# Context projection drawn into a state-space layer, state sums put ahead of a convolution, and a small copy put first in a chunk

## The chip, the cores and the metric

The kernel runs on one core of a Trainium2 chip. The metric is device time in microseconds (us), the median of several executions. A core has five engines with one instruction queue each: TensorE (PE, matrix products, results in PSUM), VectorE (DVE), ScalarE (ACT), GpSimd (POOL) and SyncE (SP, which here only issues DMA transfers). Engines run side by side and wait for each other by semaphores; within one queue the order is fixed.

## The reference, cut to what matters

All arrays are float32. The image x has 2 batches of 128 channels of 64x64 positions. Four layers follow each other:

- Layer 0: a layer norm over channels, then four Mamba passes over the 4096 tokens of each batch (row order forward and backward, column order forward and backward), each with a projection to 256 channels, a causal convolution of four taps, a scan over 16 states, a gate and an output projection; the four outputs are fused and added to x.
- Layer 1: attention of each position over a context picture, and a 3x3 convolution of the result, added to x.
- Layer 2: attention of x over itself, added to x.
- Layer 3: a small Mamba over groups of 16 channels, a group norm, and an addition.

The context has 4 pictures of 256 channels of 32x32. It is resized bilinearly to 2 pictures of 64x64 and then multiplied by Wk and Wv:

```python
ctx = jax.image.resize(context_feat, (B, Cc, H, W), method='bilinear')
q = conv2d(sr_feat, Wq, bq, 0).reshape(B, C, H * W)
k = conv2d(ctx, Wk, bk, 0).reshape(B, C, H * W)
v = conv2d(ctx, Wv, bv, 0).reshape(B, C, H * W)
```

Resizing and projecting are both linear. The kernel therefore first mixes the 4 pictures to 2 (weights 3/7, 3/7, 1/7 and 1/7, 3/7, 3/7), projects at 32x32, and resizes the 128 projected channels in height and width last. The context does not depend on x.

## The kernel before, in words

**Layer 0.** The work is cut into 64 chunks of 512 tokens: batch, then order (row or column), then direction, then 8 pieces. Chunk k has 16 steps; step u treats one group of 4 states (u%8//2) and one quarter of the 256 channels. The channels of a quarter and its states fill 128 partitions, so a step works on 128x1024. In each step POOL forms dbu (L330), ACT the decay da (two halves, L343), a correction of the first token (s_fix, L358) and the carried state (s_hst, L379); DVE scans (s_scan, L374); the product with C is on DVE (s_hc, L386), in five of the sixteen steps on POOL (L384); PE sums over states (s_y, L397) and spreads C over partitions (s_pc, L363).

Around the steps lies what prepares other chunks. For the chunk after next: px, the projection with the convolution folded in, as four shifted products (L228), in two halves px(0) and px(1), each copied out by ACT (x_, L237), and then pd (L267), which makes the 73 rows of the inputs of dt, B and C. For the next chunk: xd_ (L272), which copies these 73 rows out of PSUM and stores B and C to DRAM, pt (L287), dt and its product (L306, L314), and the gate's projection pz (L241). For the chunk before: the gate product yg(0) and yg(1) (L404) and the output projection po (L415, L419). For later chunks, in 11 chunks, a layer norm: center, sub, square, var, rows, scale, mul, affine. In 16 chunks ACT transposes a strip of the normed tokens (turn, L201) from xn to xnt, which the column-order chunks read.

The order is written out by hand. For each chunk the dictionaries A (ACT), V (DVE), M (PE) and G (POOL) say what is issued in which step besides the fixed work, and the loop over s issues it. A norm goes on in a chunk where ln is not None (it begins) or lp is not None (it ends). The results of px, pz, pd, pt, center, var, scale and po share one PSUM bank (misc), so each must be copied out before the next may start. y has one bank as well; y0 starts it at steps 3 and 11.

**The crossing to layer 1.** Behind the last chunk, weights m1 and m2 are loaded on SP (L682, L683), the product of two weight matrices wvo and a bias bo are formed (L705 to L710), the four context pictures are loaded (L726), mixed on DVE (L731 to L733), projected in 32 PE records (L740), copied out by ACT (L742), and stored with doubled edge rows to DRAM (L746).

**Layers 1 and 2.** Four jobs (layer, batch) of 16 groups of 256 queries are run through 16 slots each, as a pipeline: scores of one group (L847), probabilities and values (L902) of the one before, sums of the one before that. A key piece or a value piece of 1024 positions is made from the low picture by a load (L799), a wide part on ACT and POOL (L804 to L813) and a high part on ACT and POOL (L818 to L824); value pieces are also transposed on PE (L785). The first two key pieces come before the first slot, the others at slots given to piece.

Of the kernel before, what the change touches and what calls it, by code (L numbers as in the profile page):

```python
# [13 lines left out]
P = 128  # L14
B, C, H, W = 2, 128, 64, 64
L = H * W
T = 512
# [39 lines left out]
def conv_seq_kernel(ctx: ExitStack, tc: tile.TileContext, a: dict, out: bass.AP):  # L57
# [13 lines left out]
    for b in range(B):  # L71
        for lo, hi in ((0, 1), (1, 2), (2, 4), (4, 8)):
            sl = slice(lo * T, hi * T)
            nc.sync.dma_start(x[:, b, sl], xin[:, b, sl])
# [14 lines left out]
    nc.vector.tensor_scalar(aneg, aneg, -1.0, None, ALU.mult)  # L89

# [3 lines left out]
    with ExitStack() as c0:  # L94
# [22 lines left out]
        nc.scalar.dma_start(w_dt[64:ND, :], a["wdt"])  # L117
        w_xT, w_out, w_fT = mt[:, 0:256], mt[:, 256:512], mt[:, 512:1024]
# [21 lines left out]
        for t in (xn, xnt):  # L140
            nc.vector.memset(t[:, 0:3], 0.0)
            nc.vector.memset(t[:, L + 3 : L + 6], 0.0)

# [292 lines left out]
        turns = {k: k % 8 for k in (*range(6, 14), *range(32, 40))}  # L436
# [6 lines left out]
        with tc.manual_schedule():  # L443
# [64 lines left out]
            for i in range(2):  # L508
                nc.vector.tensor_scalar(diag_d[:, i, :], ident, v(f"dp{i}"), None, ALU.mult)
            for j in (2, 3):  # L510
                act(sqs[j], xcs[j], AF.Square)
# [20 lines left out]
            nc.vector.reciprocal(r[:, 8:16], r[:, 8:16])  # L532
            for i in range(2):
                c1.px(i, ba[i])
# [21 lines left out]
            for k, c in enumerate(chunks):  # L556
# [15 lines left out]
                if new is not None:  # L572
                    A[0] = (new.xd_,)
# [9 lines left out]
                if nxt is not None:  # L583
                    M[8], A[9] = lambda: nxt.px(0), (lambda: nxt.x_(0),)
                    M[10], A[12] = lambda: nxt.px(1), (lambda: nxt.x_(1),)
                    A[13] = (nxt.xsilu,)
                    M[15] = nxt.pd
                if lp is not None:
# [3 lines left out]
                    A[10] = (lp.affine,)  # L592
                if ln is not None:
                    M[12], V[13] = ln.center, ln.sub
                    A[14] = (*A.get(14, ()), ln.square)
                    M[14], A[15] = ln.var, (ln.keep,)
                if k in turns:
                    A[11] = (lambda: turn(turns[k]),)

                for s in range(16):  # L600
# [11 lines left out]

                    if c1 is not None:
# [7 lines left out]
                    if s in (3, 11):  # L621
                        c.y0(s // 11)
                    for cy, e in ((c, s), (old, s + 16)):
                        for u in pairs.get(e, ()) if cy is not None else ():
                            cy.s_y(u)
                            cy.s_y(u + 1)
# [35 lines left out]
    nc.sync.dma_start(m3, a["m3"])  # L662
    nc.sync.dma_start(cw3, a["cw3"].partition_broadcast(P))
    nc.sync.dma_start(dtw3, a["dtw3"].partition_broadcast(P))
# [4 lines left out]
    with ExitStack() as c1:  # L669
# [8 lines left out]
        dr = c1.enter_context(tc.tile_pool(name="dr1", bufs=1, space=bass.MemoryType.DRAM))  # L678

        m1 = gt([P, 1792], "m1", wp)  # L680
        m2 = gt([P, 512], "m2", wp)
        nc.sync.dma_start(m1, a["m1"])  # L682
        nc.sync.dma_start(m2, a["m2"])  # L683
        w1qT = m1[:, 0:128]
        w1kT = m1[:, 128:384].rearrange("p (k c) -> p k c", k=2)
        w1vT = m1[:, 384:640].rearrange("p (k c) -> p k c", k=2)
# [12 lines left out]
        def small(tag, shape, bufs=None):  # L699
# [4 lines left out]
        pw = misc()  # L704
        mm(pw[:, :P], lhsT=w2v, rhs=w2oT, start=True, stop=True)  # L705
        nc.vector.tensor_copy(wvo, pw[:, :P])
        bo = gt([P, 1], "bo", wp)
        pw = misc()
        mm(pw[:, :1], lhsT=w2oT, rhs=v("bv2"), start=True, stop=True)
        nc.vector.tensor_add(bo, v("bo2"), pw[:, :1])  # L710
# [6 lines left out]


        low = [[dr.tile([P, 34, 32], F32, tag=f"low{b}{w}", name=f"low{b}{w}") for w in range(2)]
               for b in range(B)]  # L720
        cfeat = a["ctx"].rearrange("b (k p) h w -> p b k (h w)", p=P)
        with ExitStack() as cc:
            cx = cc.enter_context(tc.tile_pool(name="ctx", bufs=1))
# [3 lines left out]
            for b in range(B):  # L727

                wts = (3 / 7, 3 / 7, 1 / 7) if b == 0 else (1 / 7, 3 / 7, 3 / 7)
                mix = cx.tile([P, 2, 1024], F32, tag="mix", name="mix", bufs=2)  # L730
                nc.vector.tensor_scalar(mix, feat[b], wts[0], None, ALU.mult)  # L731
                nc.vector.scalar_tensor_tensor(mix, feat[b + 1], wts[1], mix, ALU.mult, ALU.add)
                nc.vector.scalar_tensor_tensor(mix, feat[b + 2], wts[2], mix, ALU.mult, ALU.add)  # L733

                for w, (wT, bias) in enumerate(((w1kT, v("bk1")), (w1vT, v("bv1")))):
                    t = cx.tile([P, 34, 32], F32, tag="lo", name="lo", bufs=2)
                    for hf in range(2):
                        pl = bank("s", bufs=4)
                        for k in range(2):
                            mm(pl, lhsT=wT[:, k, :], rhs=mix[:, k, hf * T : (hf + 1) * T],  # L740
                               start=(k == 0), stop=(k == 1))
                        act(t[:, 1 + 16 * hf : 17 + 16 * hf, :], pl.rearrange("p (h w) -> p h w", w=32),  # L742
                            AF.Identity, bias=bias)
# [804 lines left out]
```

## Time and profile before

The median of 3 runs is 6803.33 us (6800.08 to 6806.97). The profiled execution took 6810.44 us.

| | us |
|---|---|
| span of the profiled execution | 6808.7 |
| busy PE, DVE, ACT, POOL | 6005.6, 5524.3, 4461.8, 5362.4 |
| first scan of layer 0 | 57.15 |
| last matmul of layer 0 ends | 3480.54 |
| first score of layer 1 | 3523.67 |

The busy time is a sum over stages that are limited by different engines, so it has to be read by stage. In a row of the clock-ordered view, the first number is the start in microseconds from the start of the span, the second the duration of what the row gathers, then come engine, line, operation, the tiles written and read, and in brackets how long the engine was idle before and what released it. In a row of the view of waits, the three numbers are the sum, how often, and the longest, in microseconds.

### The profile page before, as it was taken

The page shows a single profiled execution, that of the slowest core. Times are in us where ns is not written, and L with a number is a line of the kernel's source. Part 1 is how long each engine was busy: PE and PEld are TensorE (multiplying, and loading weights), DVE is VectorE, ACT ScalarE, POOL GpSimd, SP SyncE. Part 2 cuts the span into 40 slices and gives each one's busy share as a digit, 9 for nine tenths or more (in the row PEclk, how much of TensorE's full clock was granted, in tenths as well). Part 3 has the DMA queues.
Part 4 walks back from the last instruction along what each step waited for, and adds up shares of the span by engine and source line. Part 5 has one row for each costly group of instructions (what it writes and reads, how often), then busy time and mean ns, then how long its engine had stood idle before and what let it go on. Part 6 is the DMA issues. An engine that isn't in the chain of part 4 may idle for free. (4 is left out here: it accounts for less than half of the span.)

```text
span 6808.7 us, 67303 instructions
## 1 busy us (share of the span) xinstructions
PE 6005.6 (88%) x20652; PEld 2821.7 (41%) x20652; DVE 5524.3 (81%) x4499; ACT 4461.8 (66%) x7666; POOL 5362.4 (79%) x2487
## 2 busy tenths in 40 slices
PE   8888888888888888888879999999999997888888
PEld 2222222222222222222238887787788884222222
DVE  7999999999999999999966665565566675787777
ACT  7887778877788777887745664555456564434342
POOL 6899998899999999999956664555566666777776
PEclk7777777777778777777779999999999998988888
DMA  6565655566566656665630000000000001222221
GB/s 170 138 149 145 157 145 140 137 154 150 141 159 152 157 143 154 150 154 146 148 93 2 4 4 1 1 1 1 1 1 13 1 1 61 75 71 72 90 75 67
DMA packets 352652, 616.51 MB, mean 91 GB/s; under 512 B 72473, under 2 KB 74786, under 8 KB 351650
## 3 DMA queue, kind: packets, MB, share of 16 engines
q1 hardware_dynamic: 351552, 610.44, 35.2%
q8 instruction: 162, 2.65, 0.2%
q14 instruction: 200, 1.64, 0.1%
q10 hardware_dynamic: 738, 1.78, 0.1%
HBM read 496.45 MB, written 115.47 MB: 90 GB/s over the span
## 5 line engine op out<-in xcount | busy, mean ns | idle before, releaser
L330 POOL TENSOR_TENSOR dbu<-dus,bs 128x1024 f32<-128x1024 f32 x1024 | 2404.0, 2374 | 157.0 <-DVE h L374 141.1
L374 DVE TENSOR_TENSOR_SCAN h<-da,hst,dbu 128x1024 f32<-128x1024 f32 x896 | 2094.3, 2345 | 77.8 <-ACT dbu L358 75.0
L343 ACT ACTIVATE da<-dts,aneg 128x512 f32<-128x512 f32 (+1 forms) x2048 | 1412.6, 690 | 443.7 <-DVE h L374 404.1
L890 POOL TENSOR_TENSOR sum<-sum,sc 128x1024 f32<-128x1024 f32 x384 | 906.8, 2362 | 496.7 <-ACT sc L885 493.1
L852 ACT COPY sc<-s 128x512 f32<-128x512 f32 x1024 | 598.1, 585 | 867.7 <-PE s L847 753.5
L859 DVE TENSOR_TENSOR mx<-mx,s 128x512 f32<-128x512 f32 x896 | 610.1, 681 | 569.5 <-ACT sc L852 568.5
L847 PE MATMUL s<-q,k 128*128 128x256 f32 x4096 | 1058.0, 382 | 11.7 <-ACT q L833 8.4
L902 PE MATMUL av<-sc,v 128*128 128x256 f32 x4096 | 1049.6, 379 | 2.3 <-ACT sc L885 2.3
L397 PE MATMUL y<-hc,cst 128*32 128x512 f32 x4096 | 811.3, 760 | 179.2 <-DVE hc L386 103.8
L386 DVE TENSOR_TENSOR hc<-h,pc 128x1024 f32<-128x1024 f32 x704 | 844.9, 1200 | 0.1
L847 PEld LDWEIGHTS s<-q,k 128*128 128x128 f32 x4096 | 781.2, 192 | 146.2 <-issue 36.6
L902 PEld LDWEIGHTS av<-sc,v 128*128 128x128 f32 x4096 | 769.1, 190 | 103.1 <-ACT sc L885 3.7
L384 POOL TENSOR_TENSOR hc<-h,cs 128x1024 f32<-128x1024 f32 x320 | 758.2, 2369 | 1.3 <-issue 1.3
L363 PE MATMUL pc<-xd,sel 16*128 16x512 f32 x1024 | 713.4, 788 | 4.8 <-DVE hc L386 4.1
L1217 POOL TENSOR_TENSOR A<-A,D 128x1024 f32<-128x1024 f32 x224 | 525.9, 2365 | 225.2 <-DVE D L1222 200.3
L882 DVE TENSOR_TENSOR sc<-sc,pm 128x1024 f32<-128x1024 f32 x512 | 620.9, 1214 | 0.9 <-PE pm L878 0.9
L885 ACT ACTIVATE sc<-sc 128x1024 f32<-128x1024 f32 x512 | 542.3, 1059 | 8.6 <-DVE sc L882 8.1
L287 PE MATMUL misc<-xd,w_dt 9*128 9x512 f32 x504 | 386.5, 855 | 155.1 <-ACT x L426 83.6
L1210 ACT ACTIVATE A<-dtr,aneg 128x1024 f32<-128x1024 f32 (+1 forms) x256 | 246.0, 1032 | 380.8 <-PE y L1242 363.0
L397 PEld LDWEIGHTS y<-hc,cst 128*32 128x32 f32 x4096 | 104.9, 117 | 745.6 <-issue 337.4
L1228 DVE TENSOR_TENSOR A<-A,q 128x1024 f32<-128x1024 f32 (+1 forms) x256 | 276.9, 1082 | 148.4 <-PE q L1194 148.2
L1194 PE MATMUL q<-xs,lb 32*128 32x512 f32 x896 | 331.5, 712 | 72.0 <-DVE D L1204 65.7
(263 smaller groups left out, 8078.4 us busy)
## 6 DMA issues: line engine op xcount, KB each, us to landing
dts<-ddt SPq DMA_DIRECT2D x512, 256.0 KB, 5.5
dus<-ddu SPq DMA_DIRECT2D x512, 256.0 KB, 5.1
bs<-rows SPq DMA_DIRECT2D x1024, 64.0 KB, 4.9
cs<-rows SPq DMA_DIRECT2D x1024, 64.0 KB, 3.3
ddt<-dt SPq DMA_DIRECT2D x128, 256.0 KB, 2.0
ddu<-dtu SPq DMA_DIRECT2D x128, 256.0 KB, 4.1
dtr<-ddt SPq DMA_DIRECT2D x448, 64.0 KB, 1.9
rx<-ddx SPq DMA_DIRECT2D x448, 64.0 KB, 1.9
```

The lines of the kernel that those rows point to most:

```text
L330: nc.gpsimd.tensor_mul(t, self.dus[q], _bc(self.bs[g], 1, [P, 2, T]))
L343: act(t[:, i, sl], self.dts[q][:, i, sl], AF.Exp, scale=an[:, g, 2 * q + i : 2 * q + i + 1])
L363: mm(t, lhsT=sel[32:48, 4 * g : 4 * g + 4, :].rearrange("p n d -> p (n d)"), rhs=self.xd[32:48, :], start=True, stop=True)
L374: nc.vector.tensor_tensor_scan(ho, ai, bi, init, ALU.mult, ALU.add)
L384: nc.gpsimd.tensor_mul(t, self.h[u], _bc(self.cs[gq(u)[0]], 1, [P, 2, T]))
L386: nc.vector.tensor_mul(t, self.h[u], _bc(self.pc[u // 2], 1, [P, 2, T]))
L397: mm(self.y[q // 2][r : r + 32, :], lhsT=sum4, rhs=self.hc[u][:, i, :], start=False, stop=(u % 8 >= 6), skip_group_check=True)
L847: mm(p[:, o, :], lhsT=j.k[m // 8][:, m % 8 * P : m % 8 * P + P], rhs=self.q, start=True, stop=True)
L859: nc.vector.tensor_max(self.mx, self.s[0][:, 0:2, :] if u == 1 else self.mx, self.p[u])
L882: nc.vector.tensor_sub(s, s, _bc(self.pm[:, :], 1, [P, 4, NQ]))
L890: nc.gpsimd.tensor_add(self.sum, self.s[0] if w == 1 else self.sum, self.s[w])
L902: mm(self.av, lhsT=self.job.v[m // 8][:, m % 8, :], rhs=self.s[u // 2][:, m % 4, :], start=(m == 0), stop=(m == 31))
```

## The change

1. The context is loaded in the opening of layer 0, into buffers not yet in use: the first and last picture into xnt, the two middle ones into buffers of h and dbu. DVE mixes them there in place (`mixed`). Four chunks, 7 to 10, each project one batch for keys or values in two halves on PE through the misc bank (`Low`), ACT copies each out, and SP stores it to DRAM. The weights and outputs of this stand in the space of x[:, 1], which is loaded at the tops of chunks 11 to 14 instead of in the opening. The turns of the first batch come two chunks later.
2. Of the crossing there remain the loads of m1 and m2, now behind or between the loads of the first two key pieces, and the making of key pieces. The other steps are removed or, for wvo, bo and layer 3's weights, moved to slots 50 to 52 of the attention. The resizes for the first batch's keys use DVE instead of POOL. Later key pieces begin one slot earlier; value pieces begin two slots earlier, with their transposes at the same slots as before.
3. In every chunk of layer 0, px(0) is issued in step 9 instead of 8, and x_(0) in step 10. The text of y0 and the sums stands ahead of ACT's work, which changes no order within a queue.
4. In step 0 of chunks in which no norm ends, xd_ is issued ahead of the decay, the fix and the carry.

```diff
-    for b in range(B):
-            nc.sync.dma_start(x[:, b, sl], xin[:, b, sl])
+        nc.sync.dma_start(x[:, 0, sl], xin[:, 0, sl])
...
+        w_kv = x[:, 1, 0:512].rearrange("p (w k c) -> p w k c", w=2, k=2)
+        nc.scalar.dma_start(x[:, 1, 0:512], a["m1"][:, 128:640])
...
+        cfeat = a["ctx"].rearrange("b (k p) h w -> p b k (h w)", p=P)
+        mix = [[xnt[:, 3 + 1024 * (2 * b + k) : 1027 + 1024 * (2 * b + k)] for k in range(2)]
+               for b in range(B)]
+        feat = {}
+        for k in range(2):
+            nc.sync.dma_start(mix[0][k], cfeat[:, 0, k])
+        for j in (1, 2):
+            for k in range(2):
+                feat[j, k] = wt("h" if j == 1 else "dbu", NH if j == 1 else NDBU, (P, 1024))
+                nc.sync.dma_start(feat[j, k], cfeat[:, j, k])
+        for k in range(2):
+            nc.sync.dma_start(mix[1][k], cfeat[:, 3, k])
+
+        def mixed(b):
+            w = (3 / 7, 3 / 7, 1 / 7) if b == 0 else (1 / 7, 3 / 7, 3 / 7)
+            for k in range(2):
+                m = mix[b][k]
+                nc.vector.tensor_scalar(m, m, w[0 if b == 0 else 2], None, ALU.mult)
+                for j in (1, 2):
+                    nc.vector.scalar_tensor_tensor(m, feat[j, k], w[j - b], m, ALU.mult, ALU.add)
+
+        class Low:
...
+            def conv(self):
+                self.p = misc()
+                for k in range(2):
+                    mm(self.p, lhsT=w_kv[:, self.w, k, :], rhs=mix[self.b][k][:, self.hf * T : self.hf * T + T],
+                       start=(k == 0), stop=(k == 1))
+
+            def out(self):
+                t = x[:, 1, T * (1 + self.hf) : T * (2 + self.hf)]
+                act(t, self.p, AF.Identity, bias=v("bv1" if self.w else "bk1"))
+                o = low[self.b][self.w].rearrange("p h w -> p (h w)")
+                nc.sync.dma_start(o[:, 32 + T * self.hf : 32 + T * self.hf + T], t)
+                if self.hf:
+                    nc.sync.dma_start(o[:, 33 * 32 :], t[:, T - 32 :])
+                else:
+                    nc.sync.dma_start(o[:, 0:32], t[:, 0:32])
...
-        turns = {k: k % 8 for k in (*range(6, 14), *range(32, 40))}
+        turns = {k: k % 8 for k in (*range(8, 16), *range(32, 40))}
...
             for i in range(2):
                 nc.vector.tensor_scalar(diag_d[:, i, :], ident, v(f"dp{i}"), None, ALU.mult)
+            mixed(0)
...
             nc.vector.reciprocal(r[:, 8:16], r[:, 8:16])
+            mixed(1)
...
-                    A[0] = (new.xd_,)
+                    if lp is not None:
+                        A[0] = (new.xd_,)
...
-                    M[8], A[9] = lambda: nxt.px(0), (lambda: nxt.x_(0),)
+                    M[9], A[10] = lambda: nxt.px(0), (lambda: nxt.x_(0),)
...
-                    A[10] = (lp.affine,)
+                    A[10] = (lp.affine, *A.get(10, ()))
...
+                if 7 <= k < 11:
+                    w1, w2 = (Low((k - 7) // 2, (k - 7) % 2, hf) for hf in range(2))
+                    M[6], A[7] = w1.conv, (w1.out,)
+                    M[13], A[14] = w2.conv, (w2.out, *A.get(14, ()))
+                if 11 <= k < 15:
+                    sl = slice(2 * T * (k - 11), 2 * T * (k - 10))
+                    nc.sync.dma_start(x[:, 1, sl], xin[:, 1, sl])
...
+                    if s in (3, 11):
+                        c.y0(s // 11)
+                    for cy, e in ((c, s), (old, s + 16)):
+                        for u in pairs.get(e, ()) if cy is not None else ():
+                            cy.s_y(u)
+                            cy.s_y(u + 1)
+
+                    if s == 0 and new is not None and lp is None:
+                        new.xd_()
                     if c1 is not None:
                         c1.s_da(u1)
                         c1.s_fix(u1)
...
-                    if s in (3, 11):
-                        c.y0(s // 11)
-                    for cy, e in ((c, s), (old, s + 16)):
-                        for u in pairs.get(e, ()) if cy is not None else ():
-                            cy.s_y(u)
-                            cy.s_y(u + 1)
...
-        nc.sync.dma_start(m1, a["m1"])
-        nc.sync.dma_start(m2, a["m2"])
...
+        def second():
+            pw = misc()
+            mm(pw[:, :P], lhsT=w2v, rhs=w2oT, start=True, stop=True)
+            nc.vector.tensor_copy(wvo, pw[:, :P])
+
+        def second_bias():
+            pw = misc()
+            mm(pw[:, :1], lhsT=w2oT, rhs=v("bv2"), start=True, stop=True)
+            nc.vector.tensor_add(bo, v("bo2"), pw[:, :1])
...
-            feat = [cx.tile([P, 2, 1024], F32, tag=f"ct{j}", name=f"ct{j}") for j in range(4)]
-            for j in range(4):
-                nc.sync.dma_start(feat[j], cfeat[:, j])
...
-                    for hf in range(2):
-                        pl = bank("s", bufs=4)
...
-                nc.sync.dma_start(low[b][w], t)
...
+                eng = nc.vector if self.b == 0 and w == 0 else nc.gpsimd
...
-                        nc.gpsimd.tensor_add(o[:, :, :, e], st["lo"], st["q"][:, :, 2 * e : 2 * e + 32])
+                        eng.tensor_add(o[:, :, :, e], st["lo"], st["q"][:, :, 2 * e : 2 * e + 32])
...
-                        nc.gpsimd.tensor_add(o[:, :, e, :], st["t"], st["hz"][:, 2 * e : 2 * e + 8, :])
+                        eng.tensor_add(o[:, :, e, :], st["t"], st["hz"][:, 2 * e : 2 * e + 8, :])
...
+        def thirds():
+            nc.sync.dma_start(m3, a["m3"])
+            nc.sync.dma_start(cw3, a["cw3"].partition_broadcast(P))
+            nc.sync.dma_start(dtw3, a["dtw3"].partition_broadcast(P))
...
-            for qd in range(2):
-                for f in jobs[0].key_piece(qd):
-                    f()
-            piece(1, jobs[0], "key_piece", 2)
-            piece(5, jobs[0], "key_piece", 3)
+            k0, k1 = (jobs[0].key_piece(qd) for qd in range(2))
+            k0[0]()
+            nc.sync.dma_start(m1[:, 0:128], a["m1"][:, 0:128])
+            k1[0]()
+            nc.sync.dma_start(m1[:, 128:], a["m1"][:, 128:])
+            nc.sync.dma_start(m2, a["m2"])
+            for f in k0[1:]:
+                f()
+            groups[0].q = jobs[0].query(0)
+            for f in k1[1:]:
+                f()
+            piece(0, jobs[0], "key_piece", 2)
+            piece(4, jobs[0], "key_piece", 3)
             for qd in range(4):
-                piece(10 + 5 * qd, jobs[0], "value_piece", qd)
-            groups[0].q = jobs[0].query(0)
+                piece(8 + 5 * qd, jobs[0], "value_piece", qd, 2)
+            put(50, second, thirds, second_bias)
```

More of the change, by code (lines that the diff above doesn't have):

```diff
@@ L70, in conv_seq_kernel @@
     xin = a["x"].rearrange("b c h w -> c b (h w)")
-    for b in range(B):
-        for lo, hi in ((0, 1), (1, 2), (2, 4), (4, 8)):
-            sl = slice(lo * T, hi * T)
-            nc.sync.dma_start(x[:, b, sl], xin[:, b, sl])
+    for lo, hi in ((0, 1), (1, 2), (2, 4), (4, 8)):
+        sl = slice(lo * T, hi * T)
+        nc.sync.dma_start(x[:, 0, sl], xin[:, 0, sl])
     nc.scalar.dma_start(vec, a["vec"])
@@ L89, in conv_seq_kernel @@
     nc.vector.tensor_scalar(aneg, aneg, -1.0, None, ALU.mult)
+    drc = ctx.enter_context(tc.tile_pool(name="drc", bufs=1, space=bass.MemoryType.DRAM))
+    low = [[drc.tile([P, 34, 32], F32, tag=f"low{b}{w}", name=f"low{b}{w}") for w in range(2)]
+           for b in range(B)]
     with ExitStack() as c0:
@@ L142, in conv_seq_kernel, with __init__ @@
             nc.vector.memset(t[:, L + 3 : L + 6], 0.0)
+        cfeat = a["ctx"].rearrange("b (k p) h w -> p b k (h w)", p=P)
+        mix = [[xnt[:, 3 + 1024 * (2 * b + k) : 1027 + 1024 * (2 * b + k)] for k in range(2)]
+               for b in range(B)]
+        feat = {}
[15 more added lines that the diff above has]
+        class Low:
+            def __init__(self, b, w, hf):
+                self.b, self.w, self.hf = b, w, hf
+            def conv(self):
[12 more added lines that the diff above has]
+                    nc.sync.dma_start(o[:, 0:32], t[:, 0:32])
         def gq(u):
@@ L661, in conv_seq_kernel @@
     dtw3 = gt([P, 32], "dtw3", late)
-    nc.sync.dma_start(m3, a["m3"])
-    nc.sync.dma_start(cw3, a["cw3"].partition_broadcast(P))
-    nc.sync.dma_start(dtw3, a["dtw3"].partition_broadcast(P))
     with ExitStack() as c1:
@@ L677, in conv_seq_kernel @@
         ps = c1.enter_context(tc.tile_pool(name="ps1", bufs=1, space=PSUM))
-        dr = c1.enter_context(tc.tile_pool(name="dr1", bufs=1, space=bass.MemoryType.DRAM))
         m1 = gt([P, 1792], "m1", wp)
         m2 = gt([P, 512], "m2", wp)
-        nc.sync.dma_start(m1, a["m1"])
-        nc.sync.dma_start(m2, a["m2"])
         w1qT = m1[:, 0:128]
-        w1kT = m1[:, 128:384].rearrange("p (k c) -> p k c", k=2)
-        w1vT = m1[:, 384:640].rearrange("p (k c) -> p k c", k=2)
         w1pT = m1[:, 640:1792].rearrange("p (k c) -> p k c", k=9)
@@ L703, in conv_seq_kernel @@
         wvo = gt([P, P], "wvo", wp)
-        pw = misc()
-        mm(pw[:, :P], lhsT=w2v, rhs=w2oT, start=True, stop=True)
-        nc.vector.tensor_copy(wvo, pw[:, :P])
         bo = gt([P, 1], "bo", wp)
-        pw = misc()
-        mm(pw[:, :1], lhsT=w2oT, rhs=v("bv2"), start=True, stop=True)
-        nc.vector.tensor_add(bo, v("bo2"), pw[:, :1])
+        def second():
[6 more added lines that the diff above has]
+            nc.vector.tensor_add(bo, v("bo2"), pw[:, :1])
         gbp = gt([P, 1], "gbp", wp)
@@ L716, in conv_seq_kernel @@
         nc.gpsimd.memset(pad, 0.0)
[L719 to L723, printed above, removed]
-            feat = [cx.tile([P, 2, 1024], F32, tag=f"ct{j}", name=f"ct{j}") for j in range(4)]
-            for j in range(4):
-                nc.sync.dma_start(feat[j], cfeat[:, j])
[L727 to L736, printed above, removed]
-                    for hf in range(2):
-                        pl = bank("s", bufs=4)
[L739 to L743, printed above, removed]
-                    nc.scalar.copy(t[:, 0:1, :], t[:, 1:2, :])
-                    nc.scalar.copy(t[:, 33:34, :], t[:, 32:33, :])
-                    nc.sync.dma_start(low[b][w], t)
         sp_ = c1.enter_context(tc.tile_pool(name="s", bufs=13))
@@ L953, in put, with piece @@
                 todo.setdefault(slot + i, []).append(f)
-        def piece(slot, j, what, qd):
+        def piece(slot, j, what, qd, later=0):
             steps = []
@@ L963, in piece @@
             n = 2 if j.layer == 2 else 7 if what == "value_piece" else 5
-            put(slot, first, *[lambda i=i: steps[i]() for i in range(1, n)])
+            put(slot, first, *[lambda i=i: steps[i]() for i in range(1, min(n, 5))])
+            put(slot + 5 + later, *[lambda i=i: steps[i]() for i in range(5, n)])
         for n, j in enumerate(jobs):
```

## The prediction, on record before the changed kernel ran

> **What bounds the kernel now.** I read the busy row of the page first, then the busy time by stretches, then the waits of each engine inside layer 0, then the clock-ordered records where a wait stood out. By stretches (columns: length; busy time of PE, PEld, DVE, ACT, POOL; granted clock; DMA share; GB/s) two chunk-loop and attention stretches read:
>
> ```profile
> 2000.00:3480.00 1480.00, 1258.68 (x3322) 337.60 (x3318) 1429.48 (x869) 1172.76 (x2226) 1429.66 (x642) 0.76 0.60 147
> ...
> 3640.00:4000.00 360.00, 346.44 (x1645) 301.86 (x1645) 248.85 (x304) 218.18 (x343) 231.66 (x120) 1.00 0.01 3
> ```
>
> Layer 0 (up to 3480) is held by DVE and POOL together, both at 97%; PE is at 85%, at three quarters of its clock. Attention is held by PE (96%). So in the loop only idle time of DVE or POOL is worth anything. What DVE waits for in all of the loop (165 to 3480):
>
> ```profile
> DVE h L374 <- ACT dbu L358: 73.9, 127, 1.4
> DVE dt L404 <- PE y L397: 37.7, 35, 2.4
> ```
>
> With 19.3 us more before L404 that have no releaser, the gate product L404 waits 57.0 us in all: 24.3 in front of yg(0) in the 11 chunks in which a norm goes on, 14.3 in front of yg(1) in the others, the rest scattered. The scan's wait for L358 is ACT coming late with decay and carry.
>
> The third place is the crossing from layer 0 to layer 1, where PE waits (3480 to 3640):
>
> ```profile
> PE misc L785 <- POOL up L824: 11.2, 4, 4.1
> PE s L740 <- DVE mix L733: 9.6, 1, 9.6
> PE misc L705 <- DMA m<-in_m_dram: 7.8, 1, 7.8
> PE s L847 <- ACT q L833: 7.0, 1, 7.0
> ```
>
> In clock order (start, duration, engine, line):
>
> ```profile
> 3499.68 16.60 PE L740 MATMUL s<-mix,m 128*128 128x512 f32 x32 [9.64 <-DVE mix L733]
> ...
> 3509.72 0.34 SPq L799 DMA_DIRECT2D lo<-low  x1
> ...
> 3523.67 6.67 PE L847 MATMUL s<-q,k 128*128 128x256 f32 x18 [6.96 <-ACT q L833]
> ```
>
> Layer 0's last matmul is at 3480.54, the first score at 3523.67: 43 us of weights, context loads, mixing, 16.6 us of projection at half clock, a trip through DRAM and two resizes. Every later group follows from that first score.
>
> [...] the same eight matmuls of a convolution half take 5.64 us in px(0) and 3.70 in px(1) of one chunk. [...]
>
> **The change, part by part.** All sums are against the profiled execution: 6810.4 us, span 6808.7.
>
> *Crossing.* Weights, wvo and bias, mixing, projection, eight 0.69 us outputs, the edge copies and stores leave it. What remains: the key load goes at 3480.6, when SP comes free of layer 0 as now. From L799 to the first ACT operation took 2.29 us (3509.72 to 3512.01): 3482.9. Wide part on ACT 0.47+0.20+0.21+0.47, some 1.2 as in the second piece (3517.93 to 3519.11): 3484.1. Two 128x320 adds, on DVE now[...] (POOL took 1.59). High part on ACT 0.63+0.74: 3486.5. Two 128x512 adds at 0.69: 3487.9 (POOL took 2.49). The query needs m1[:,0:128], second on SP, landing about 3483.5, and is ready earlier. First score 3488.0 for 3523.7: **-35.7**. After it, PE waited 14.5 us more for resizes on POOL (11.2 above, 3.3 for the second key piece). Keys now take 2.4 us of DVE in place of 4.1 of POOL, and value resizes begin two slots (3.8 us of a 30.56 us group of 16) sooner with POOL free of keys. I take 3 us as left: **-11.5**. wvo and the bias move to slots 50 to 52, where PE is the bound: 0.77+0.59: **+1.4**. The three small loads of layer 3 move on SP with nothing behind them: 0. Crossing **-46**; bounds -35 (all 14.5 stay[...]) and -51 (nothing stays).
>
> *Opening.* Out: 2 MB of x[1]. In: eight context loads (4 MB) and 256 KB of weights, so 2.25 MB more. The loads of before are all down by 18.6 us at about 400 GB/s; now by about 24. DVE is idle for 14.5 us up to 38.1 (L306), and 6.3 us up to 46.2. One mix is half of the crossing's rows, (1.22+2.29+2.29) = 5.8 us; both fit. One more issue on ACT's queue, 0.4 us: **+1**; without cover, 12.
>
> *Projection in chunks 7 to 10.* Eight PE records more a chunk (3.4 us warm, 6.8 cold), two ACT outputs (1.4) and four stores on SP. PE has 15% spare but the one misc bank hands on px, pz and pt in a row, and an out is ahead of the decay on ACT. I take 1 us a chunk (0 to 3): **+4**. The x[1] loads at the tops of chunks 11 to 14 are issued at once, 0.4 us of SP; what is behind them on SP lands 5 us after issue with slots of slack. Turns two chunks later keep their 1.1 us: 0.
>
> *Sums ahead of px(0).* px(0) goes from slot 8 to 9 and behind s_y(6), s_y(7); x_(0) from ACT's slot 9 to 10. In a norm chunk:
>
> ```profile
> 1234.55 5.64 PE L228 MATMUL misc<-xnt,wk 128*128 128x512 f32 x8
> ...
> 1241.31 0.69 DVE L404 TENSOR_TENSOR dt<-sz,y 128x512 f32<-128x512 f32 x1 [2.46 <-issue]
> ```
>
> The sums waited at PE behind px(0); now they end about 1236.5 and yg(0) waits for nothing. But px(0) then ends at about 1241.0, px(1) about when it did (1242.1), and behind it the norm's center, which is only 0.6 us early for its subtraction. So of 2.2 us about half returns: 11 chunks x -1.1 = **-12**. In the 19 forward chunks without a norm, yg(0) waits little (0.17) and the order costs: at 2794 to 2847 the product hc(7) ends at 2825.7, sums to 2826.7, px(0) at 5.2 cold to 2831.9; x_(0) stands on ACT ahead of da(12), which moves from 2829.6 to 2832.5, and scan(12) from 2833.03 to 2834.3. +1.3 cold, -0.7 warm, mean +0.6: **+12**. In the 31 reverse chunks +0.3 to +0.6, which lies inside a 1.0 us wait for POOL that they have at step 5: 0.
>
> *Small copy first.* In 52 chunks xd_ (0.68 us, and two row stores on SP) goes ahead of s_da(1), s_fix(1) and the last carry. xd_ waits for PE's pd, and all ACT work waits behind it. Here:
>
> ```profile
> 701.15 4.59 DVE L374 TENSOR_TENSOR_SCAN h<-da,hst,dbu 128x1024 f32<-128x1024 f32 x2 [0.64 <-ACT dbu L358]
> ...
> 702.41 3.69 PE L267 MATMUL misc<-xs,m 128*73 128x512 f32 x4
> ...
> 706.14 0.68 ACT L272 ACTIVATE xd<-misc,vec 73x512 f32<-73x512 f32 x1 [0.40 <-PE misc L267]
> ...
> 706.77 2.35 DVE L374 TENSOR_TENSOR_SCAN h<-da,hst,dbu 128x1024 f32<-128x1024 f32 x1
> ```
>
> the scan ends at 703.5 and da(1) starts at once; now it starts at 706.8, needs 1.8 with its fix, and scan(1) (706.77) is 1.9 us late. That is pd at its longest (3.69 cold; 1.94 warm). Over all chunks pd ends 0 to 2.9 us after the scan, and scan(1) has 1.1 to 1.5 us to spare: with the pd times of before the stalls sum to 45.7 us. Of that 14.3 take the place of yg(1) waits, since pt(0) and with it the sums come sooner, and about 13 fall in the POOL wait of step 5: +18. With px(0) later [...] pd may be warm: then 0. I take a third: **+6** (-10 to +45).
>
> Sum: -46+1+4-12+12+6 = **-35**: 6775.4 profiled. The median of the runs, 6803.33, lies 7.1 below the profiled time, so **6768**.
>
> **Rivals.**
> (1) The forecast: crossing gained, loop about even; 6748 to 6788. 0.55.
> (2) The loop gains as well: pd warm throughout, all of L404's 57 us goes and little comes back, say -30 more: 6735, down to 6715. For it: DVE is the bound and those waits are the largest that the edits touch. Against it: POOL at 97% leaves no more than 3% of 3315 us. 0.15.
> (3) The loop eats the gain: pd cold, stalls of 25 to 45 us: 6790 to 6810, hardly to be told from 6803. The example just shown speaks for it. 0.20.
> (4) Slower: the copy queued ahead of decay waits for pd in all 52 chunks and scan(1) slips by the same each time. It decides from (46+14)/52 = 1.2 us a chunk; the example has 1.9, giving 52 x 1.9 = 99 less 46 = about 6850. Against it: the mean raw stall is 0.9. 0.06.
> (5) The crossing keeps its later waits (-35) or mixing isn't covered (+12): 6780 to 6790. 0.04.
>
> **How the numbers follow.** A measurement of this kernel tells about 0.2% (13.6 us) from no change, 6789.7 to 6816.9. Faster holds (1), (2), (5) and a little of (3): 0.77; same most of (3) and a sliver of (4): 0.16; slower 0.07. The range leaves out about one in ten at each end: 6730 to 6806.
>
> **What would show it.** Right: the first score 34 to 38 us sooner after layer 0's last matmul; no L705 or L740 wait, L785's down to a few us; yg(0) unstalled in norm chunks; layer 0 within 15 us of its length. Wrong: a new wait of ACT L272 for PE of over 60 us, with the scan's wait for L358 grown well above 73.9; reverse chunks longer than 52.5 us; forward chunks with scan(12) late; or DVE waiting in the opening for context. The error most likely is PE's clock ahead of pd and in px(0), which the trace of before can't give for another order.

## The result and the profile after

The changed kernel takes 6745.6 us (median of 6 runs, 6742.64 to 6756.56); the kernel before took 6803.97 beside it. The ratio is 0.992 with a 95% interval of 0.9907 to 0.9933: 58 us less, where 35 were forecast. The profiled execution went from 6810.44 to 6743.73 us, its span from 6808.7 to 6741.9.

The program has three stages that can be read apart. The first ends with layer 0's last matmul, the second with the start of the last group's query (L831 before, L864 after), the third with the span.

| stage, us of the profiled execution | before | after | change |
|---|---|---|---|
| layer 0 | 3480.5 | 3474.1 | -6.4 |
| crossing and attention | 2130.0 | 2076.4 | -53.6 |
| last group and layer 3 | 1198.2 | 1191.4 | -6.8 |

Nothing that runs in the third stage was edited. Over the twelve experiments below it took between 1183 and 1206 us, with nothing in it changed either, so its -6.8 is scatter; the comparisons below are therefore made by stage where a few microseconds count. Layer 0 scatters too: in the last two kernels below (keys back on POOL, pieces back at their old slots), which change only the crossing, the same layer 0 ends at 3482.0 and 3465.9, 8 us to either side of the changed kernel's 3474.1. A difference of less than 16 us between two profiles' layer 0 therefore says little.

The stretches of the changed kernel that answer to the two shown of before (columns: length; busy time of PE, PEld, DVE, ACT, POOL; granted clock; DMA share; GB/s):

```profile
2000.00:3440.00 1440.00, 1215.86 (x3224) 326.46 (x3220) 1382.13 (x842) 1137.29 (x2169) 1409.06 (x625) 0.79 0.62 150
3600.00:3960.00 360.00, 345.02 (x1636) 300.31 (x1636) 245.67 (x301) 217.87 (x345) 232.82 (x124) 1.00 0.01 3
```

POOL is now busier than DVE in layer 0 (98% and 96%). What DVE waits for there (165 to 3440), the four largest:

```profile
DVE h L427 <- ACT dbu L411: 88.8, 125, 1.8
DVE dt L457 <- PE y L450: 10.6, 11, 1.4
DVE xc L214 <- PE misc L210: 9.9, 9, 1.5
DVE hc L439 <- PE y L450: 7.4, 14, 0.9
```

The gate product's wait fell from 57.0 us (two releasers together) to 10.6; there are new waits of 9.9 for the norm's center and 7.4 for the sums. What is left of the gate product's wait stands in front of yg(1), and only in chunks in which a norm ends: these are the chunks in which the small copy still stands behind the decay. PE's waits at the crossing (3474 to 3600) are all small:

```profile
PE s L864 <- ACT q L837: 3.6, 1, 3.6
PE s L880 <- DVE k L857: 3.3, 1, 3.3
PE pm L911 <- DVE sc L915: 2.3, 2, 1.3
PE s L880 <- DVE mx L892: 1.8, 3, 1.2
PE misc L817 <- POOL up L857: 1.4, 1, 1.4
```

In clock order, the crossing after:

```profile
3474.24 0.34 SPq L832 DMA_DIRECT2D lo<-low  x1
...
3477.87 0.89 DVE L846 TENSOR_TENSOR hz<-lo,q 128x320 f32<-128x320 f32 x2 [3.57 <-DMA lo<-low]
...
3480.22 1.29 DVE L857 TENSOR_TENSOR k<-h,hz 128x512 f32<-128x512 f32 x2 [1.46 <-ACT hz L852]
...
3481.62 9.41 PE L880 MATMUL s<-q,k 128*128 128x256 f32 x32 [3.29 <-DVE k L857]
```

The first score comes 7.5 us after layer 0's last matmul, in place of 43.1.

The same moments of a norm chunk:

```profile
1165.52 3.70 PE L281 MATMUL misc<-xnt,wk 128*128 128x512 f32 x8
...
1168.34 0.66 DVE L457 TENSOR_TENSOR dt<-sz,y 128x512 f32<-128x512 f32 x1
...
1177.90 0.69 DVE L214 TENSOR_TENSOR xc<-x,misc 128x512 f32<-128x512 f32 x1 [1.04 <-PE misc L210]
```

px(0) takes 3.70 us and not 5.64, yg(0) has no wait, and the only loss is 1.04 us in front of the norm's subtraction.

Why px(0) is shorter is read from the clock that PE was granted (third number from the end; 1.00 and 0.50 are what the prediction calls warm and cold). Before, where px(0) began at 1234.55:

```profile
1221.50:1238.40 16.90, 14.67 (x31) 3.99 (x24) 16.90 (x12) 12.86 (x26) 16.82 (x9) 0.50 0.57 167
1238.60:1255.40 16.80, 14.40 (x48) 4.13 (x46) 13.78 (x10) 14.09 (x26) 14.07 (x7) 1.00 0.68 160
```

After, where it began at 1165.52:

```profile
1151.60:1165.10 13.50, 10.93 (x26) 2.52 (x26) 13.50 (x10) 11.64 (x24) 13.50 (x7) 0.50 0.48 128
1165.20:1185.60 20.40, 17.62 (x64) 6.16 (x60) 19.11 (x12) 17.55 (x36) 20.11 (x10) 1.00 0.90 214
```

Before, px(0) began 4 us ahead of the return to the full clock; after, it begins just behind it. Over the 11 norm chunks it began 1.1 to 4.4 us ahead before and begins 0.15 to 0.45 us behind now. In both kernels, in all 11, PE has no pause directly ahead of px(0). The lengths of these chunks go with this. In the two traces the granted clock changes 451 and 385 times, and the stretches between changes were all whole multiples of 3.413 us; the last three norm chunks took 17 of these before (57.99, 58.01 and 58.02 us) and take 16 now (54.60, 54.61 and 54.61), and with dbu at its old place, in a kernel below, the same. So the gain of a norm chunk looks like one such unit. That loop and clock keep step with each other is the author's estimate from these lengths; no experiment here shows it.

A reverse chunk:

```profile
2460.54 1.94 PE L320 MATMUL misc<-xs,m 128*73 128x512 f32 x4
...
2460.76 4.59 DVE L427 TENSOR_TENSOR_SCAN h<-da,hst,dbu 128x1024 f32<-128x1024 f32 x2 [1.26 <-ACT dbu L411]
...
2462.82 0.68 ACT L325 ACTIVATE xd<-misc,vec 73x512 f32<-73x512 f32 x1
...
2466.39 2.34 DVE L427 TENSOR_TENSOR_SCAN h<-da,hst,dbu 128x1024 f32<-128x1024 f32 x1
```

pd is over by 2462.5, before the first scan of the next chunk begins, so the copy that now goes first waits for nothing, and scan(1) at 2466.39 has no wait.

Chunk lengths, from the first scan of a chunk to that of the next, summed by kind, as change against the kernel before. The norm chunks are 1 to 4 and 16 to 22; the forward ones 5 to 7, 32 to 39 and 48 to 55; the reverse ones 8 to 15, 24 to 31, 40 to 47 and 56 to 62. The last column is the end of layer 0:

| kernel | 11 norm chunks | 19 forward | 31 reverse | end of layer 0, us |
|---|---|---|---|---|
| before | 630.7 us | 1001.6 us | 1629.8 us | 3480.5 |
| changed | -29.1 | +9.2 | +13.0 | 3474.1 |

The norm chunks gained more than twice what was forecast. The others lost 22 us, which is what the forecast's terms for them come to as well (12, 6 and 4), but POOL's dbu, 16 of them a chunk, went from 2374 to 2437 ns, which no step of the forecast had. The experiments are about these points.

### The profile page after: what moved, and what is told of

It reads as the page before. It is cut to its first block, busy times and chain, and to the rows that moved or that the text cites. A ratio compares the mean times of both kernels' runs of the same rounds, so it can differ in the third digit from the quotient of the medians.

```text
span 6741.9 us, 67309 instructions
## 1 busy us (share of the span) xinstructions
PE 5957.8 (88%) x20652; PEld 2794.8 (41%) x20652; DVE 5535.0 (82%) x4521; ACT 4446.2 (66%) x7658; POOL 5393.9 (80%) x2471
## 5 line engine op out<-in xcount | busy, mean ns | idle before, releaser
L383 POOL TENSOR_TENSOR dbu<-dus,bs 128x1024 f32<-128x1024 f32 x1024 | 2458.0, 2437 | 100.1 <-DVE h L427 85.5
L450 PE MATMUL y<-hc,cst 128*32 128x512 f32 x4096 | 880.2, 755 | 196.0 <-DVE hc L439 176.1
L340 PE MATMUL misc<-xd,w_dt 9*128 9x512 f32 x504 | 371.3, 824 | 145.0 <-ACT x L479 79.6
L450 PEld LDWEIGHTS y<-hc,cst 128*32 128x32 f32 x4096 | 125.3, 120 | 852.9 <-DVE hc L439 414.5
L411 ACT ACTIVATE dbu<-hst,dbu,df 128x1 f32<-128x1 f32 x896 | 337.9, 377 | 82.5 <-POOL dbu L383 60.2
```

The lines of the kernel that those rows point to most:

```text
L383: nc.gpsimd.tensor_mul(t, self.dus[q], _bc(self.bs[g], 1, [P, 2, T]))
L450: mm(self.y[q // 2][r : r + 32, :], lhsT=sum4, rhs=self.hc[u][:, i, :], start=False, stop=(u % 8 >= 6), skip_group_check=True)
```

## The experiments

**The two edits of the loop, alone and together.** First, px(0) late only where a norm goes on:

```diff
-                    M[9], A[10] = lambda: nxt.px(0), (lambda: nxt.x_(0),)
+                    es = 9 if ln is not None or lp is not None else 8
+                    M[es], A[es + 1] = lambda: nxt.px(0), (lambda: nxt.x_(0),)
```

> The changed kernel with px(0) back in step 8 and x_(0) in step 9 in chunks in which no norm begins or ends; the new order stays in the norm chunks. The 11 norm chunks became 29.2 us shorter in the changed kernel, the other 51 about 21 us longer. Theory A (the later px(0) is what makes the others longer): 10 to 20 us below the changed kernel, 6726 to 6736, and the wait of DVE's product in step 13 for the sums gone. Theory B (they are longer because POOL's dbu takes 2.437 us there against 2.374 before, 16 of them a chunk): within 5 us of the changed kernel, 6741 to 6751, with dbu still at 2.44.

Measured: 6749.4 us (4 runs; ratio to before 0.9924, 0.9909 to 0.9939), layer 0 ending at 3482.1. dbu stayed at 2.44. The time speaks for theory B, against A: taking the late px(0) out of the other chunks gained nothing, though the wait of DVE's product for the sums in step 13 is gone from the reverse chunks. Layer 0 stands 8 us above the changed kernel's, as it does in the kernel with the keys back on POOL, whose layer 0 is the changed kernel's own; this is scatter. One new wait is large all the same:

```profile
DVE h L427 <- ACT hst L432: 48.2, 33, 2.7
```

It is taken up below, where the four combinations are compared.

Then the small copy behind the decay again:

```diff
-                    if lp is not None:
-                        A[0] = (new.xd_,)
+                    A[0] = (new.xd_,)
...
-                    if s == 0 and new is not None and lp is None:
-                        new.xd_()
```

> The changed kernel with xd_ behind the decay again in all chunks. The forecast's step (the copy first costs about 6 us, mostly where pd is late): 6735 to 6742. Rival (it pays, since the rows and pt come sooner and yg(1) no longer waits): 6755 to 6762, with waits in front of yg(1) of some 14 us back in the chunks without a norm.

Measured: 6772.2 us (4 runs; 0.9958, 0.9943 to 0.9973), layer 0 at 3499.9. The rival was right, and by more than it said: the copy first is worth some 26 us in the changed kernel, where I had forecast a cost.

And px(0) in step 8 in all chunks:

```diff
-                    M[9], A[10] = lambda: nxt.px(0), (lambda: nxt.x_(0),)
+                    M[8], A[9] = lambda: nxt.px(0), (lambda: nxt.x_(0),)
```

> The changed kernel with px(0) in step 8 and x_(0) in step 9 in all chunks. Theory A (sums first gains 29 in norm chunks and costs about 20 in the others): 6750 to 6760. Theory B (the others' loss is POOL's): 29 us longer, 6770 to 6778. In both px(0) of the norm chunks takes 5.4 us again, not 3.70, and yg(0) waits some 24 us.

Measured: 6786.9 us (7 runs; 0.9977, 0.9966 to 0.9989), layer 0 at 3511.6; slower even than theory B had it. In the norm chunks px(0) takes 5.34 us again (3.70 in the changed kernel, 11 of 11) and DVE waits 24.3 us for yg(0), as said. But a wait stands there that neither theory named, the second line of DVE's waits in layer 0:

```profile
DVE h L427 <- ACT dbu L411: 68.9, 126, 1.7
DVE h L427 <- ACT hst L432: 45.6, 33, 2.6
```

It is scan(1), which waits 41.7 us in the 28 reverse chunks behind chunk 10. With the copy first and px(0) early, pd lasts 3.07 us there on the mean and comes late: ACT stands at the copy, and the decay behind it. This is the stall that the forecast had worked out as 45.7 us over all chunks.

With both edits undone, by the same lines, what is left is the context part and the crossing:

> The kernel before with the context part and the crossing alone: order of sums and of the small copy as before. Crossing -53.5, opening +0.7, projection +4 to +5 by the trace of the changed kernel: 6752 to 6760 if nothing else hangs on it. If POOL's slower dbu comes with the context part, it is about 20 us more, 6770 to 6780, and its dbu shows 2.44 us; if the dbu is back at 2.37 the slowness came with the other two edits or with the chip.

Measured: 6773.3 us (5 runs; 0.9965, 0.9951 to 0.9979), layer 0 at 3509.9, dbu at 2.444 us. So the slow dbu comes without the two edits. The four combinations, in layer 0, with the first of these kernels as a fifth row:

| | end of layer 0 | norm | forward | reverse |
|---|---|---|---|---|
| context alone | 3509.9 | +3.1 | +6.7 | +18.2 |
| + copy first | 3511.6 | +0.5 | +9.1 | +19.3 |
| + sums first | 3499.9 | -28.1 | +10.6 | +36.4 |
| + both | 3474.1 | -29.1 | +9.2 | +13.0 |
| + copy first, sums first in norm chunks only | 3482.1 | -26.8 | +8.9 | +19.8 |

The copy first alone costs 2 us and the sums first alone bring 10; both lie within the scatter, and the medians against the kernel before give a cost of 14 and a gain of 1. Both together bring 36 by layer 0 and 29 by the medians, which is clear of it.

The rows say where this comes from. The norm chunks gain some 30 us by the sums first, with the copy first or without it. The reverse chunks lose 18 by the sums first where the copy is not first: DVE waits 30.5 us there in front of yg(1) in step 1 (the 28 chunks behind chunk 10). The copy first removes this wait, and none of it is left in these chunks of the changed kernel, since PE can have pt(0) sooner and with it the sums queued behind pt(0).

The other direction is weaker. The sums first make pd short: 1.94 us in 26 or 27 of these 28 chunks where they are first in all chunks, 2.91 to 3.16 on the mean in the other three rows. But the copy first hardly needs that. In the last row pd is long (3.16) and scan(1) waits 43.2 us in these 28 chunks, yet the reverse chunks are within 2 us of those with the context alone. The stall takes the place of other waits: all of DVE's idle time in the 28 chunks is 62.7 us with the context alone, 66.5 with the copy first, 67.0 in the last row and 58.5 with both. The wait in step 5 alone falls from 32.8 with the context alone to 8.1 and 7.0 in the two rows with the stall. In the second row, too, a stall of 41.7 us costs almost nothing.

**Where POOL's time went.** The context part takes buffers of dbu in the opening. In these kernels tiles lie in the order in which their names first appear, so dbu moved from byte 208032 of each partition's memory to 130144, right behind hc, and what lay behind it moved up by 12288. The next kernel is the one before with this shift and no other change:

```diff
+        for _ in range(NDBU):
+            nc.vector.memset(wt("dbu", NDBU, (P, 1024))[:, 0:1], 0.0)
```

> The kernel before with three tiles of dbu taken in the opening, each with one column set to zero and not used further. This changes nothing but where tiles lie: dbu moves from 208032 bytes into each partition's memory to 130144, and what lies behind it (bs, dus and others) up by 12288, just as in the changed kernel. Theory P (the place of the tiles makes POOL's dbu slow): dbu takes 2.44 us, not 2.37, and the kernel is 15 to 30 us slower than before, 6818 to 6832. Rival (the chip or the moved context work makes it slow): dbu 2.37 here if it is the context work, 2.44 in no case but the chip's; time within 8 us of before.

Measured: 6821.3 us (15 runs) against 6806.0; ratio 1.0017, 1.0008 to 1.0026, so slower by 5 to 18 us. Its profiled execution, at 6846.3 us, was the longest of the 15, 25 above their median; in it layer 0 ends 28 us later than in that of before, at 3508.7, so the size of the loss is better taken from the ratio. The group of the page for dbu, which had 2374 ns (columns: busy time, mean ns, idle before and its releaser):

```profile
L332 POOL TENSOR_TENSOR dbu<-dus,bs 128x1024 f32<-128x1024 f32 x1024 | 2462.4, 2441 | 133.1 <-DVE h L376 117.9
```

Theory P holds. Its counterpart is the changed kernel with the old places, brought about by taking tiles in the old order in the opening:

```diff
+        for tag, n, shape in (("xc", 1, (P, T)), ("sq", 1, (P, T)), ("r16", 1, (P, 16)), ("xs0", None, (P, T)),
+                              ("xs1", None, (P, T)), ("xd", None, (ND, T)), ("bs", 4, (P, T)), ("e", 1, (P, 2, T)),
+                              ("dt", 1, (P, 2, T)), ("dts", 2, (P, 4, T)), ("dtu", 1, (P, 2, T)),
+                              ("dus", 2, (P, 4, T)), ("cs", len(GROUPS_C), (P, T))):
+            t = wt(tag, n, shape)
+            nc.vector.memset(t[0:1, 0:1, 0:1] if len(shape) == 3 else t[0:1, 0:1], 0.0)
```

> The changed kernel with thirteen tiles taken in the opening in the old order, one element of each set to zero, so that all tiles of layer 0 lie where they lay before, and nothing else changed. Theory P: dbu back at 2.37 us, layer 0 shorter by 15 to 25 us, 6718 to 6732, below both kernels. Rival: dbu still 2.44, time within 6 us of the changed kernel's 6746.

Measured: 6726.2 us (4 runs, 6721.44 to 6728.28); ratio 0.9884, 0.9868 to 0.99. It beats both kernels: 80 us below the kernel before beside it, and 19 below the changed kernel's median. Layer 0 ends at 3451.0, 23 us before the changed kernel's.

```profile
L389 POOL TENSOR_TENSOR dbu<-dus,bs 128x1024 f32<-128x1024 f32 x1024 | 2400.0, 2367 | 128.5 <-DVE h L433 112.1
```

The norm chunks keep their gain (-28.0 against before), the forward ones stand at -1.9, the reverse ones at +1.0. So the losses of +9.2 and +13.0 in the changed kernel are the place of the tiles, not the two edits.

Which tile it is, four kernels tell, all of them the changed kernel with another order in the same list. First dbu low with bs, dus, dts and cs at their old places:

```diff
+        for tag, n, shape in (("dbu", NDBU, (P, 2, T)),
+                              ("xc", 1, (P, T)),
+                              ("sq", 1, (P, T)),
+                              ("r16", 1, (P, 16)),
+                              ("bs", 4, (P, T)),
+                              ("e", 1, (P, 2, T)),
...
+                              ("cs", len(GROUPS_C), (P, T)),
+                              ("xs0", None, (P, T)),
+                              ("xs1", None, (P, T)),
+                              ("xd", None, (ND, T))):
```

> The changed kernel with tiles taken in the opening so that bs (146592), e, dt, dts, dtu, dus (183456) and cs lie where they lay in the kernel before, dbu (130144) lies where it lies in the changed kernel, and xs0, xs1 and xd take dbu's old place at 208032. If POOL is slow because of where it writes (dbu), dbu's mean stays at 2.44 us and the time near 6746. If it is slow because of where it reads (dus, bs), the mean is 2.37 and the time near 6726.

Measured: 6751.5 us (3 runs), layer 0 at 3479.8:

```profile
L399 POOL TENSOR_TENSOR dbu<-dus,bs 128x1024 f32<-128x1024 f32 x1024 | 2460.9, 2441 | 104.9 <-DVE h L443 86.6
```

With its inputs at their old places and its output low it took 2.441 us, not the 2.367 of all tiles at their old places: the slowness went with the output's place. With dus and dts exchanged:

```diff
...
+                              ("dt", 1, (P, 2, T)),
+                              ("dus", 2, (P, 4, T)),
+                              ("dtu", 1, (P, 2, T)),
+                              ("dts", 2, (P, 4, T)),
+                              ("cs", len(GROUPS_C), (P, T)),
+                              ("dbu", NDBU, (P, 2, T))):
```

> The old places with dus and dts exchanged (dus at 162976, dts at 183456), dbu at its old place. If only dbu's place matters, POOL's mean stays 2.37 us and the time near 6726. If dus' place matters, something between 2.37 and 2.44.

Measured: 6731.3 us (2 runs), dbu 2.366 us. With bs and cs exchanged:

```diff
...
+                              ("xd", None, (ND, T)),
+                              ("cs", len(GROUPS_C), (P, T)),
+                              ("e", 1, (P, 2, T)),
...
+                              ("dus", 2, (P, 4, T)),
+                              ("bs", 4, (P, T)),
+                              ("dbu", NDBU, (P, 2, T))):
```

> The old places with bs and cs exchanged (bs at 199840, cs at 146592), dbu at its old place. If only dbu's place matters, POOL's mean stays 2.37 us; if bs' place matters it differs by 0.02 us or more.

Measured: 6724.0 us (2 runs), dbu 2.366 us. In these two kernels the places of what it reads made no difference (2.367 us with all at their old places). Last, dbu in the middle:

```diff
...
+                              ("dt", 1, (P, 2, T)),
+                              ("dbu", NDBU, (P, 2, T)),
+                              ("dts", 2, (P, 4, T)),
...
+                              ("cs", len(GROUPS_C), (P, T))):
```

> The changed kernel with dbu at 162976 to 175264, between its two places so far (130144, slow; 208032, fast); dts, dtu, dus and cs lie 12288 higher than in the kernel before. If only the low place is slow, the mean of dbu is 2.37 us and the time near 6726; if only the high place is fast, 2.44 us and near 6746; a value in between says that it goes with the distance.

Measured: 6723.8 us (2 runs), layer 0 at 3450.8:

```profile
L399 POOL TENSOR_TENSOR dbu<-dus,bs 128x1024 f32<-128x1024 f32 x1024 | 2400.5, 2368 | 128.6 <-DVE h L443 112.0
```

Of the three places only the lowest was slow: 2.427 to 2.448 us on the mean against 2.366 to 2.374. In every kernel with dbu there, six small tiles that the product neither reads nor writes have moved too. Of these xs0, xs1 and xd lie in different places in the kernel with dbu low alone and in the changed kernel, where dbu is equally slow (2.441 and 2.437 us); xc and sq are used by the norms and r16 in the opening, and dbu is slow in the last 40 chunks (2.448 us in the changed kernel) without any norm.

Why the low place is slow stays open. Within the changed kernel's loop dbu's time goes neither with the bytes that the DMA queues move at the same time (correlation -0.05) nor with the share of it that overlaps a scan (0.02). The first two dbu, in the opening, do not settle whether the loop's load is needed: they take 2.337 to 2.342 us at the two faster places, and anything from 2.338 to 2.427 us at the low one (2.357 and 2.338 in the changed kernel, 2.389 and 2.427 in the kernel with the sums first in norm chunks only).

**The crossing.** The keys back on POOL:

```diff
-                eng = nc.vector if self.b == 0 and w == 0 else nc.gpsimd
+                eng = nc.gpsimd
```

> The changed kernel with the keys resized on POOL as before. From the end of layer 0's last matmul to the first score 7.5 us in the changed kernel, by the rows of POOL and DVE 1.9 more here, 9.4. To the seventh query 139.2 us in the changed kernel (192.6 before): the forecast's reading, that POOL's queue of resizes holds the transposes, says 5 to 12 more; the rival, that the value pieces' earlier start is what counts, says 2 to 3 more.

Measured: 6754.2 us (2 runs). The first score comes 9.65 us after layer 0 (7.5 in the changed kernel). The query that the expectation calls the seventh is the sixth, with the times that it gives: 144.5 us, 5.3 more than in the changed kernel, the low end of the first reading; 2.1 of it is the later first score. But PE waits on POOL for keys, not for transposes:

```profile
PE s L880 <- POOL k L857: 7.8, 4, 5.0
PE s L864 <- ACT q L837: 3.5, 1, 3.5
PE misc L817 <- POOL up L857: 2.0, 1, 2.0
```

The pieces back at their old slots:

```diff
-            piece(0, jobs[0], "key_piece", 2)
-            piece(4, jobs[0], "key_piece", 3)
+            piece(1, jobs[0], "key_piece", 2)
+            piece(5, jobs[0], "key_piece", 3)
             for qd in range(4):
-                piece(8 + 5 * qd, jobs[0], "value_piece", qd, 2)
+                piece(10 + 5 * qd, jobs[0], "value_piece", qd)
```

> The changed kernel with the later key pieces at slots 1 and 5 and the value pieces at 10, 15, 20 and 25 as before. First score unchanged, 7.5 us after layer 0. To the seventh query: the forecast's reading says 5 to 10 us more than 139.2, as transposes wait for POOL again; if keys on DVE are all it takes, 0 to 2 more.

Measured: 6755.5 us (2 runs). First score as in the changed kernel, sixth query 152.1 us after layer 0, 12.9 more:

```profile
PE misc L817 <- POOL up L857: 10.6, 4, 3.6
```

That wait is 1.4 in the changed kernel and 11.2 before. So the earlier slots, of key and value pieces together, are what removes the transposes' wait; keys on DVE alone do not.

## Why the prediction was right, point by point

The forecast was 6768 and the time 6746, inside the range of 6730 to 6806 and on the side called most likely; the change is -58 and not -35, just beyond the likeliest case's own lower end of 6748. The crossing was right in mechanism and came out at -53.6, a little beyond its own bound of -51. Layer 0 was forecast at +11 and measured at -6, and that it came so near is luck: some of its terms missed by about 20 us and more, in both directions. The terms:

- *First score.* Forecast 35.7 us sooner, measured 35.6 (43.1 to 7.5). From the load to ACT it took 2.34 us (2.29 in the forecast), and the two pairs of adds on DVE took 0.89 and 1.29 us. For the second pair the forecast had twice 0.69, as the trace of before has it for a 128x512 add (L859, 0.69); its price of the first pair was shown by no trace of before, which has no 128x320 add on DVE. Alone, such an add took 0.49 us in the changed kernel and one of 128x512 0.69; a pair took 0.08 to 0.09 us less than two, because by the trace the second began that much before the first had ended. The prediction says of the old projection that its 16.6 us ran at half clock; that is misread. The granted clock was 0.61 in its first 6.8 us and 1.00 in the rest. The sum does not hang on it.
- *Waits after it.* Forecast -11.5, with 14.5 us as all there was to win. Measured -18 (2130.0 to 2076.4, less the first score). From the first score to the sixth query PE's idle time fell by 10 us (18.0 to 8.1), near the forecast. Its busy time for the same work fell by 8 more (131.5 to 123.6), with a mean granted clock of 0.98 in place of 0.91. The failed step is the list of what could go: it held only the waits for POOL's resizes and had no term for PE running slowly. By the sixth query, 12.9 us hang on the earlier pieces and 3.2 on keys on DVE, besides the 2.1 of the first score.
- *Opening.* Forecast +1, first scan 57.15 to 57.91. The cover was there.
- *Projection.* Forecast +4. Chunks 7 to 10 together took 1.6 to 1.7 us more than before in the four kernels whose dbu is not slow. These have the other edits as well, so this is an estimate: the term was about 2 us too large, inside its own bounds. The eight records of a chunk took 5.39 to 5.77 us in the changed kernel, between the 3.4 warm and 6.8 cold of the prediction; the records of the old projection followed each other every 0.43 us at a granted clock of 1.00 and every 0.85 at 0.50.
- *Sums first, norm chunks.* Forecast -12, measured -31 beside the context part alone. The failed step is the length of px(0) in its new place: the forecast let it end at about 1241.0 and px(1) "about when it did", so it took px(0) to last nearly as long as before. In the changed kernel it takes 3.70 us in all 11 norm chunks (5.37 on the mean before), and so does it where only this edit stands. The sum has no term for the granted clock, though the prediction shows px(0) and px(1) of one chunk at 5.64 and 3.70 us. In the trace the shorter px(0) goes with the clock: it begins 0.15 to 0.45 us behind the return to the full clock and not 1.1 to 4.4 us ahead of it, with no pause of PE directly ahead in either order.
- *Sums first, other chunks.* Forecast +12 in forward ones, measured +3.9 beside the context part alone and +0.1 beside context and copy; px(0) there fell from 4.96 to 3.92 us, so the warm end of the forecast's +1.3 to -0.7 was the likelier. In reverse chunks forecast 0, measured +18 for this edit alone: the wait at step 5 was not the only one, as yg(1) came to wait in step 1.
- *Copy first.* Forecast +6 as a third of +18. The stall of 45.7 us that it started from is real (41.7 with px(0) early, in 28 chunks), but alone it made the reverse chunks only 1 us longer. The failed step is what hides it: "about 13 fall in the POOL wait of step 5" was too little, as that wait gave up 25 (32.8 to 8.1). And the gain was put at 14.3 us of old waits only, not at those that the other edit brings: beside sums first the edit is worth -26, as it takes away yg(1)'s wait of 30.5. (The chunks with the copy first are 51, not 52, as the last chunk has no copy.)
- *What was not in the sum.* The place of dbu: 23 us in layer 0 between the changed kernel and that with the old places (15 to 31 by the three profiles of the same layer 0), 19 by the medians, and 5 to 18 where it was the only change. It was hidden in the result by gains that were also not foreseen. Rival 2 (the loop gains as well, 6715 to 6735) had much of the mechanism: pd short in the reverse chunks, most of the gate product's wait gone. Its "little comes back" holds only without the misplacement, where the time is 6726.

Of the prediction's signs of being wrong one came, reverse chunks longer than 52.5 us: they took 53.0 on the mean. But those of before took 52.6 already, and those of the kernel with the old places take 52.6 too, so the sign told of dbu and not of the copy.

## What to carry to other kernels

Price two edits of the same loop together, not one by one: here the sums first cost the reverse chunks what the copy first removed, and neither edit alone was clear of scatter. A stall need not be a loss: over 40 us of new waits of one scan cost almost nothing, since other waits shrank by as much. Where PE's clock changes within a loop, look at when a long matmul group begins against the return of the clock: here two short groups put ahead of it moved it across, from 5.37 to 3.70 us on the mean of 11 chunks. And when a change takes a buffer earlier than before, compare the mean times of instructions that it doesn't touch: a shift of tiles showed as 63 ns in one group of 1024, and undoing it was the next gain.

## What the runs showed of the hardware

POOL's product dbu (128x1024 float32, two inputs) took 2.366 to 2.374 us on the mean with its output at byte 162976 or 208032 of each partition, and 2.427 to 2.448 us with it at 130144, in fourteen profiles, the twelve experiments on four chips, whatever places its inputs had in these kernels. POOL's product hc, of the same shape, moved less (2.363 to 2.369 and 2.381 to 2.395 us). The loop paid only part of it: between the changed kernel and that with the old places the 1024 products differ by 72 us in all (2437 and 2367 ns), and layer 0 by 23. Where the boundary lies, and whether it has to do with the neighbours h and hc, was not tried.
